# Two preactivated attention blocks on one core: the reciprocals of layer 1's softmax sums taken in a layout of 128 rows by 8

## The chip, the core and the metric

The kernel runs on one core of a Trainium2 chip. A core has TensorE (PE) for matrix products, VectorE (DVE) and ScalarE (ACT) for elementwise work, GpSimd (POOL) and SyncE (SP), which here mostly issue DMAs, a working memory of 128 partitions (SBUF), accumulator banks (PSUM) that PE writes, and DRAM. Each engine runs its own list of instructions in order; semaphores hold an instruction back until what it needs is done. The metric is the time of one execution on the device in microseconds (us), taken as the median of several runs.

## The reference

The input x is (4, 32, 32, 768) in fp32: four images of 1024 tokens and 768 channels. Two layers follow one another, each of them `x = x + attention(group_norm(x))`, with 12 heads of 64 channels. Cut to what matters, layer 1 is

```python
q, k, v = split(group_norm(x) @ w_qkv.T + b_qkv)        # per head
q, k, v = (layer_norm(dwconv3x3(a, w_pool)) for a in (q, k, v))
attn = softmax((q * scale) @ k.T + rel_h + rel_w)        # 1024 x 1024 per head
o = attn @ v + q
x = x + o @ w_proj.T + b_proj
```

Layer 0 has the same form without the convolution, the layer norms and the `+ q`. Softmax divides each row of exponentials by its sum. The kernel does this division after the product with v: one sum for each of 1024 queries and each head.

## The kernel before, in words

**Stages, pairs, chunks.** `stages` (L164) is the order of the eight passes: image 0 layer 0, image 1 layer 0, image 0 layer 1, image 1 layer 1, and the same for images 2 and 3. Each stage has six pairs of heads, hp 0 to 5; two heads of 64 channels fill the 128 partitions. `attend` (L720) works through a pair in two chunks c of QC = 512 queries, each with eight key tiles of 128. A chunk is 8 steps, a pair 16. In each half of a chunk PE computes four tiles of scores (L820: q times k; L822: the relative position bias), ACT takes the exponentials (L827), and PE multiplies them with V (L844) into the bank `av`.

**Order.** The program is written under a manual schedule: every engine's instructions stand exactly in the order in which the code issues them. `events` (L981) is a table from step to pieces of other work: the next pair's q, k and v (products L131, convolution taps on DVE L542 and L544, layer norm with sums by PE at L556 and L591, means and variances by DVE at L559 and L570, `r_ln` by L153 to L160, scaled V at L582, bias parts at L613 to L640), the next stage's group norm (mean by PE at L330, copied by DVE at L334 as `gmean`), and the last stage's projection with its `os_sums` (L902, L923). These pieces are issued between the steps of `attend`, so the tail of one chunk is woven into the next chunk and into this other work.

**What follows a chunk.** `rest` (L718) is a list of functions still to be done for a finished chunk. `more()` (L731) takes one from it and is called four times in a chunk: after the scores of the first half (step offset 0), after its product with V (offset 2), after the scores of the second half (offset 4) and after its product (offset 6). `landed` does nothing and lets one call pass. At offset 6 the new chunk's parts are put on the list and `copy` (L739) runs: ACT copies `av` to `weighed` (L742).

**Sums in layer 1.** V's last column of each head is replaced by ones (L584), so the last row of each head in `av` (rows 63 and 127) is the sum of exponentials. This is done for all chunks of layer 1 except the kernel's last (47 chunks, `by_ones`). POOL writes these two rows to DRAM as z (L748, 2x512) and reads them back as `t`, each repeated for the 64 rows of its head (L749, 128x512). In the following chunk:

- offset 0: `landed`;
- offset 2: `sums`: `restore_last` rebuilds the missing column of the product with V (PE L763, ACT L768, two DMAs by POOL L771), then ACT copies t with an accumulated sum (L784) and takes 1/t as exp(-ln t) (L792, L793); the accumulated sums of t and of its reciprocal go to `seen`, which the kernel's end reduces (L1057) and compares with a limit;
- offset 4: `result`: DVE refines the reciprocal with one Newton step (L800, L801), multiplies `weighed` by it (L804) and adds it into q (L805), which the projection reads in the next stage.

In a stage of layer 1 that is followed by one of layer 0, or by nothing (`short`, L211), the chunks (hp 4, c 1) and (hp 5, c 0) have one more `landed` ahead of `sums`. Layer 0 and the last chunk sum the exponentials on DVE (L836, L838) and PE (L789); their ACT copy is L790, and the last chunk's missing column comes back through the `whole` product.

**Buffers.** `weighed`, `t` and `inv` have one buffer each, z in DRAM has two. `small_bank` is a pool of PSUM banks taken in turn by short products.

Of the kernel before, what the change touches and what calls it, by code (L numbers as in the profile page):

```python
# [9 lines left out]
F32 = mybir.dt.float32  # L10
F32R = mybir.dt.float32r
I32 = mybir.dt.int32
AF = mybir.ActivationFunctionType
ALU = mybir.AluOpType
AX = mybir.AxisListType
PSUM = bass.MemoryType.PSUM

P = 128
B = 4
S = 32  # L20
T = S * S
C = 768
NC = C // P
D = 64
HALF = T // 2
QC = 512
# [7 lines left out]
LN = 75  # L34
# [3 lines left out]
IDENT, GROUP, CENTRE, HEADS, ONES, WHOLE = 0, P, 2 * P, 3 * P, 3 * P + 2, 3 * P + 2 + D  # L38
# [7 lines left out]
def two_layers(ctx: ExitStack, tc: tile.TileContext, keep, x_in, wqkv, wproj, rels, windows, vrow, small, const, onehot, picks, out):  # L46
# [19 lines left out]
    nc = tc.nc  # L66
    pool = lambda name, bufs, **kw: ctx.enter_context(tc.tile_pool(name=name, bufs=bufs, **kw))
    fixed = pool("fixed", 1)
    dram = pool("dram", 1, space=bass.MemoryType.DRAM)
    xnp = pool("xnp", 1)  # L70
    wp = pool("wp", 2)
    work = pool("work", 2)
    one = pool("one", 1)
    stat = pool("stat", 3)
# [50 lines left out]
    def small_bank(name):  # L125
        return ps_small.tile([P, 512], F32, tag="small", name=name)
# [14 lines left out]
    cst = fixed.tile([P, NCONST], F32, tag="cst", name="cst")  # L141
# [5 lines left out]
    def col(c, lo=0, hi=P):  # L147
        return sm[lo:hi, c : c + 1]
# [62 lines left out]
    def short(i):  # L211

        after = (i // NC + 1) * NC
        return items[i][1] == 1 and (after == len(items) or items[after][1] == 0)
# [150 lines left out]
    ones = fixed.tile([P, 2 * P], F32R, tag="ones", name="ones")  # L365
# [5 lines left out]
    seen = fixed.tile([P, 2 * len(items) * (T // QC)], F32, tag="seen", name="seen")  # L371
# [346 lines left out]
    rest, found = [], ()  # L718

    def attend(pair, os):  # L720


        q, k, bias = pair.q, pair.k, pair.bias


        by_ones = [pair.layer and (pair.i < len(items) - 1 or c < T // QC - 1) for c in range(T // QC)]
        os.append(q)
        nonlocal found
        heads = [slice(j * D, (j + 1) * D) for j in range(2)]

        def more():  # L731
            nonlocal found
            if rest:
                found = rest.pop(0)(*found)

        for c in range(T // QC):
            cols = slice(c * QC, (c + 1) * QC)

            def copy(av, ones=by_ones[c]):  # L739

                weighed = one.tile([P, QC], F32, tag="weighed", name="weighed")
                nc.scalar.copy(weighed, av)  # L742
                if not ones:
                    return weighed, acc
                t = work.tile([P, QC], F32, tag="t", name="t", bufs=1)

                z = dram.tile([2, QC], F32, tag="z", name="z", bufs=2)
                nc.gpsimd.dma_start(z, weighed[D - 1 :: D, :])  # L748
                nc.gpsimd.dma_start(t, z.unsqueeze(1).to_broadcast([2, D, QC]))  # L749
                return weighed, t  # L750

            def restore(weighed):

                ps = small_bank("whole")
                halves(ps, cst[:, WHOLE : WHOLE + P], weighed)
                nc.scalar.copy(weighed, ps)

            def restore_last(weighed):

                ps = small_bank("last")  # L760
                odd = cst[:, WHOLE + 1 : WHOLE + P : 2]
                for h in range(2):
                    nc.tensor.matmul(  # L763
                        ps[h * D : (h + 1) * D, : QC // 2], odd, weighed[:, h * (QC // 2) : (h + 1) * (QC // 2)],
                        start=True, stop=True,
                    )
                last = one.tile([P, QC // 2], F32, tag="last", name="last")
                nc.scalar.copy(last, ps[:, : QC // 2])  # L768
                for h in range(2):
                    rows = last[h * D + D // 2 - 1 : (h + 1) * D : D // 2, :]  # L770
                    nc.gpsimd.dma_start(weighed[D - 1 :: D, h * (QC // 2) : (h + 1) * (QC // 2)], rows)  # L771

            def landed(*found):

                return found

            def sums(weighed, of, c=c, ones=by_ones[c]):

                at = 2 * (pair.i * (T // QC) + c)
                inv = work.tile([P, QC], F32, tag="inv", name="inv", bufs=1)  # L780
                if ones:
                    t = of
                    restore_last(weighed)
                    nc.scalar.activation(inv, t, AF.Copy, accum_out=seen[:, at : at + 1])  # L784
                else:
                    z = small_bank("z")
                    t = work.tile([P, QC], F32, tag="t", name="t", bufs=1)
                    for j, rows in enumerate(heads):
                        nc.tensor.matmul(z[rows, :], cst[:, ONES : ONES + D], of[:, j, :], start=True, stop=True)  # L789
                    nc.scalar.activation(t, z, AF.Copy, accum_out=seen[:, at : at + 1])  # L790

                nc.scalar.activation(inv, t, AF.Ln, bias=tiny)  # L792
                nc.scalar.activation(inv, inv, AF.Exp, scale=-1.0, accum_out=seen[:, at + 1 : at + 2])  # L793
                if pair.layer and not ones:
                    restore(weighed)
                return weighed, t, inv

            def result(weighed, t, inv, cols=cols):

                nc.vector.scalar_tensor_tensor(t, t, -1.0, inv, ALU.mult, ALU.mult)  # L800
                nc.vector.scalar_tensor_tensor(inv, t, 2.0, inv, ALU.add, ALU.mult)  # L801

                if pair.layer:
                    nc.vector.tensor_tensor(inv, weighed, inv, ALU.mult)  # L804
                    nc.vector.scalar_tensor_tensor(q[:, cols], inv, col(LN + 4), q[:, cols], ALU.mult, ALU.add)  # L805
                else:
                    nc.vector.tensor_tensor(inv, weighed, inv, ALU.mult)
                return (inv,)

            def finish(inv, cols=cols):  # L810

                nc.scalar.activation(q[:, cols], inv, AF.Identity, bias=col(pair.column(2)))

            for g in range(0, NKT, 4):
                es = []
                for kt, place in zip(range(g, g + 4), (None, place_b, place_c, None)):
                    keys = slice(kt * P, (kt + 1) * P)
                    ps = place.pair("s") if place else ps_a.tile([P, 2, 512], F32, tag="a", name="s")
                    for j, rows in enumerate(heads):
                        nc.tensor.matmul(ps[:, j, :], k[rows, keys], q[rows, cols], start=True, stop=False)  # L820
                    for j, rows in enumerate(heads):
                        nc.tensor.matmul(  # L822
                            ps[:, j, :], ones[rows, kt % 2 * P : (kt % 2 + 1) * P], bias[c][rows, kt // 2, :],
                            start=False, stop=True,
                        )
                    e = work.tile([P, 2, QC], F32, tag="e", name="e", bufs=4)
                    nc.scalar.activation(e, ps, AF.Exp)  # L827
                    es.append(e)
                other_work(behind_scores)
                more()  # L830
                if g == 0:
                    av = ps_av.tile([P, QC], F32, tag="av", name="av")
                if not by_ones[c]:
                    if g == 0:
                        acc = work.tile([P, 2, QC], F32, tag="acc", name="acc", bufs=1)
                        nc.vector.tensor_tensor(acc, es[0], es[1], ALU.add)  # L836
                    for e in es[2 * (g == 0) :]:
                        nc.vector.tensor_tensor(acc, acc, e, ALU.add)  # L838
                yield
                yield  # L840
                for t, e in enumerate(es):
                    kt = g + t
                    for j in range(2):
                        nc.tensor.matmul(  # L844
                            av[j * D : (j + 1) * D, :], pair.vt[:, kt, j * D : (j + 1) * D], e[:, j, :],
                            start=(kt == 0), stop=(kt == NKT - 1),
                        )
                other_work(behind_av)
                more()
                if g + 4 == NKT:  # L850

                    n_parts = 2 if short(pair.i) and (pair.hp, c) in ((NC - 2, 1), (NC - 1, 0)) else 1
                    rest.extend((landed,) * n_parts + (sums, result) if pair.layer else (sums, result, finish))
                    found = copy(av)
                yield
                yield
# [161 lines left out]
    for k, stage in enumerate(stages):  # L1018
        call, sums, products = project(stage, oss[k])
# [346 lines left out]
```

## Time and profile before

| | before |
|---|---|
| median of 3 runs | 3814.33 us (3814.24 to 3817.77) |
| the profiled execution's own time | 3816.61 us |
| its span, first to last instruction | 3814.6 us |
| mean granted TensorE clock | 0.997 |
| PE busy | 3749.5 us (98%) |
| DVE busy | 2467.1 us (65%) |
| ACT busy | 1786.5 us (47%) |
| POOL busy | 529.1 us (14%) |
| moved by DMA | 330.44 MB, 87 GB/s |

The profile is one execution, recorded by the hardware. A group's row gives the line, the engine, the operation, output and input with their shapes, the number of instructions, then busy time in us and the mean duration of one in ns, then how long the engine was idle just before them and what ended that idle time. A line of the list of waits names an engine, the tile and line that waited, what it waited for, and us in total, the number of times and the longest. A timeline's line gives the start in us, the duration, engine, line and tile, and in brackets the idle time before it with what ended it. Idle time of an engine costs time only if the last engine to finish has to wait because of it.

### The profile page before, as it was taken

What the parts mean: (1) busy time and instruction counts of PE and PEld (TensorE: products, weight loads), DVE (VectorE), ACT (ScalarE), POOL (GpSimd) and SP (SyncE); (2) the same over time, 40 slices, a digit from 0 to 9 for tenths busy, and PEclk for the clock granted to TensorE, in tenths of its full rate; (3) what the DMA queues carried; (4) which work ended last, traced back from release to release, by engine and by line L of the source; (5) the groups of instructions that cost most, each with busy time, mean ns of one, the idle gap of its engine ahead of it and who ended that gap; (6) DMA issues with size and microseconds to landing.
All of it is one profiled execution on the core that took longest, in us unless ns stands there. A gap on an engine that the chain in (4) does not pass through costs nothing. (4 is left out here: it accounts for less than half of the span.)

```text
span 3814.6 us, 76313 instructions
## 1 busy us (share of the span) xinstructions
PE 3749.5 (98%) x32990; PEld 1656.7 (43%) x32990; DVE 2467.1 (65%) x3068; ACT 1786.5 (47%) x2573; POOL 529.1 (14%) x964
## 2 busy tenths in 40 slices
PE   8999999999999999999999999999999999999998
PEld 4535535533344443444535445355343444434442
DVE  2566554559678877688454554445686888867874
ACT  2455434545355553455534544254442555525562
POOL 0111100111111211111200010001111112111120
PEclk9999999999999999999999999999999999999999
DMA  4344443331431223311333132523114212142123
GB/s 152 102 122 116 134 144 90 101 81 40 119 102 48 57 59 95 123 48 48 82 111 121 53 78 63 171 61 78 46 46 131 87 50 66 47 122 65 48 58 100
DMA packets 214024, 330.44 MB, mean 87 GB/s; under 512 B 50390, under 2 KB 103698, under 8 KB 213680
## 3 DMA queue, kind: packets, MB, share of 16 engines
q1 hardware_dynamic: 122912, 211.86, 17.9%
q0 software_dynamic: 90768, 113.61, 12.6%
q8 instruction: 263, 4.31, 0.5%
q14 instruction: 81, 0.66, 0.1%
HBM read 184.23 MB, written 40.10 MB: 59 GB/s over the span
## 5 line engine op out<-in xcount | busy, mean ns | idle before, releaser
L827 ACT ACTIVATE e<-s 128x1024 f32<-128x1024 f32 x768 | 775.6, 1024 | 423.7 <-PE s L822 393.6
L131 PE MATMUL qkv<-xn,wqkv_t 128*64 128x512 f32 x3648 | 816.0, 596 | 7.0 <-DVE gmean L334 2.6
L820 PE MATMUL s<-q,k 64*128 64x512 f32 x3072 | 808.7, 603 | 6.6 <-ACT e L827 3.1
L544 DVE SCALAR_TENSOR_TENSOR shared<-shared,sm 128x1056 f32<-128x1056 f32 x576 | 757.9, 1316 | 15.7
L822 PE MATMUL s<-bias,ones 64*128 64x512 f32 x1536 | 611.7, 790 | 1.1 <-DMA bias<-whole 1.0
L844 PE MATMUL av<-e,vt 128*64 128x512 f32 x2624 | 596.2, 596 | 0.0
L131 PEld LDWEIGHTS qkv<-xn,wqkv_t 128*64 128x64 f32 x3648 | 256.5, 137 | 484.0 <-issue 466.1
L640 POOL DMA_DIRECT2D bias<-high x384 | 205.6, 556 | 1794.6 <-ACT high L629 1559.7
L838 DVE TENSOR_TENSOR acc<-acc,e 128x1024 f32<-128x1024 f32 x294 | 360.0, 1225 | 114.0 <-ACT e L827 87.4
L820 PEld LDWEIGHTS s<-q,k 64*128 64x128 f32 x3072 | 279.5, 186 | 264.4 <-issue 213.3
L527 ACT ACTIVATE shared<-qkv,sm 128x512 f32<-128x512 f32 (+1 forms) x288 | 129.3, 502 | 469.7 <-PE qkv L131 469.7
L844 PEld LDWEIGHTS av<-e,vt 128*64 128x64 f32 x2624 | 185.4, 137 | 350.9 <-issue 316.8
L822 PEld LDWEIGHTS s<-bias,ones 64*128 64x128 f32 x1536 | 148.6, 187 | 185.4 <-issue 184.1
L640 POOL DMA_DIRECT2D bias<-whole x384 | 207.2, 571 | 53.2 <-DVE whole L630 46.3
L836 DVE TENSOR_TENSOR acc<-e 128x1024 f32<-128x1024 f32 x49 | 60.0, 1225 | 215.4 <-ACT e L827 206.8
L742 ACT COPY weighed<-av 128x512 f32<-128x512 f32 x96 | 56.3, 587 | 279.0 <-PE av L844 270.1
L559 DVE TENSOR_REDUCE mean<-ln_c 128x8 f32<-128x512 f32 x144 | 98.6, 685 | 106.0 <-PE ln_c L556 106.0
L771 POOL DMA_DIRECT2D weighed<-last x94 | 50.7, 541 | 679.6 <-ACT last L768 638.6
L613 PEld LDWEIGHTS rel<-q,rel 64*32 64x32 f32 x6144 | 112.1, 106 | 68.6 <-issue 63.8
L613 PE MATMUL rel<-q_t,rel 64*32 64x32 f32 x6144 | 123.6, 195 | 1.8 <-issue 1.8
L613 PE MATMUL rel<-q,rel 64*32 64x32 f32 x6144 | 122.7, 195 | 1.9 <-issue 1.9
L412 DVE TENSOR_TENSOR shared<-shared,m3m 128x512 f32<-128x512 f32 x66 | 45.3, 687 | 119.9 <-PE m3m L131 119.8
(162 smaller groups left out, 4439.0 us busy)
## 6 DMA issues: line engine op xcount, KB each, us to landing
bias<-high POOLq DMA_DIRECT2D x384, 128.0 KB, 2.9
bias<-whole POOLq DMA_DIRECT2D x384, 128.0 KB, 3.0
wqkv_t<-in_wqkv SPq DMA_DIRECT2D x78, 384.0 KB, 3.2
wqkv_t<-mixed SPq DMA_DIRECT2D x66, 384.0 KB, 3.1
wproj_t<-mixed SPq DMA_DIRECT2D x48, 384.0 KB, 3.3
wqkv_t<-in_wqkv SPq DMA_DIRECT2D x66, 192.0 KB, 2.5
xn<-in_x SPq DMA_DIRECT2D x24, 512.0 KB, 7.7
x<-in_x SPq DMA_DIRECT2D x48, 256.0 KB, 3.2
```

What stands on the lines that cost most here:

```text
L131: nc.tensor.matmul(ps[lo : lo + D], a[:, lo : lo + D], b, start=start, stop=stop, **kw)
L527: nc.scalar.activation(self.pad[s][:, rows, there : there + src.shape[2]], src, AF.Identity, bias=col(self.column(s)))
L544: nc.vector.scalar_tensor_tensor(y, window, tap, y, ALU.mult, ALU.add)
L559: nc.vector.tensor_reduce(of, heads, AX.X, ALU.add)
L613: nc.tensor.matmul(ps[lo : lo + S, k * S : (k + 1) * S].rearrange("p (b c) -> p b c", b=2), rel[rows, 2 * self.layer + i, first : first + ...
L640: nc.gpsimd.dma_start(sets, some.unsqueeze(1).to_broadcast([D // 2, 2, QC]))
L820: nc.tensor.matmul(ps[:, j, :], k[rows, keys], q[rows, cols], start=True, stop=False)
L822: nc.tensor.matmul(ps[:, j, :], ones[rows, kt % 2 * P : (kt % 2 + 1) * P], bias[c][rows, kt // 2, :], start=False, stop=True,)
L827: nc.scalar.activation(e, ps, AF.Exp)
L836: nc.vector.tensor_tensor(acc, es[0], es[1], ALU.add)
L838: nc.vector.tensor_tensor(acc, acc, e, ALU.add)
L844: nc.tensor.matmul(av[j * D : (j + 1) * D, :], pair.vt[:, kt, j * D : (j + 1) * D], e[:, j, :], start=(kt == 0), stop=(kt == NKT - 1),)
```

## The change

In layer 1's 47 chunks ACT no longer takes the reciprocal, and DVE no longer refines it. `copy` (still at offset 6) writes the two rows of sums to DRAM as before and then reads them back as `z_inv[:, 0, :]`, 1024 numbers laid out as 128 rows by 8. A new part, `invert`, takes the reciprocal on DVE into `z_inv[:, 1, :]`, sums both along the 8 into `seen`, and has POOL write the reciprocals to DRAM (`inv`) and read them back as `t`, repeated for the 64 rows of each head. The last part, `weighed_result`, is two DVE instructions: `t = weighed * t`, and q plus t times the layer norm's weight. `weighed` gets two buffers.

The parts of a layer 1 chunk are now `landed` (offset 0), `invert` with `restore_last` (offset 2), `landed` (offset 4), `weighed_result` (offset 6, so two steps later than `result`; it is issued there before the new chunk's `copy`). For (hp 5, c 1) they are `invert`, `only_restore`, `weighed_result` at offsets 0, 2 and 4. In short stages (hp 4, c 1) and (hp 5, c 0) have `landed`, `invert`, `only_restore`, `weighed_result` at offsets 0, 2, 4 and 6. Layer 0 and the last chunk are as before. The orders of PE's and SP's instructions are the same before and after; ACT loses L784, L792 and L793 of these chunks, DVE loses four instructions a chunk and gets four, and POOL's one DMA t<-z becomes three: z_inv<-z, inv<-z_inv, t<-inv.

```diff
--- before.py
+++ after.py
@@ -738,16 +738,44 @@
 
             def copy(av, ones=by_ones[c]):
 
-                weighed = one.tile([P, QC], F32, tag="weighed", name="weighed")
+                weighed = one.tile([P, QC], F32, tag="weighed", name="weighed", bufs=2)
                 nc.scalar.copy(weighed, av)
                 if not ones:
                     return weighed, acc
+                few = 2 * QC // P
+                z = dram.tile([2, QC], F32, tag="z", name="z", bufs=2)
+                z_inv = stat.tile([P, 2, few], F32, tag="z_inv", name="z_inv")
+                nc.gpsimd.dma_start(z, weighed[D - 1 :: D, :])
+                nc.gpsimd.dma_start(z_inv[:, 0, :], z.rearrange("j (p x) -> (j p) x", x=few))
+                return weighed, z_inv
+
+            def invert(weighed, z_inv, c=c):
+
+                at = 2 * (pair.i * (T // QC) + c)
+                nc.vector.reciprocal(z_inv[:, 1, :], z_inv[:, 0, :])
+                nc.vector.tensor_reduce(seen[:, at : at + 2], z_inv, AX.X, ALU.add)
+                inv = dram.tile([2, QC], F32, tag="inv", name="inv", bufs=2)
+                nc.gpsimd.dma_start(inv.rearrange("j (p x) -> (j p) x", x=z_inv.shape[2]), z_inv[:, 1, :])
                 t = work.tile([P, QC], F32, tag="t", name="t", bufs=1)
-
-                z = dram.tile([2, QC], F32, tag="z", name="z", bufs=2)
-                nc.gpsimd.dma_start(z, weighed[D - 1 :: D, :])
-                nc.gpsimd.dma_start(t, z.unsqueeze(1).to_broadcast([2, D, QC]))
+                nc.gpsimd.dma_start(t, inv.unsqueeze(1).to_broadcast([2, D, QC]))
                 return weighed, t
+
+            def invert_and_restore(*found, invert=invert):
+
+                found = invert(*found)
+                restore_last(found[0])
+                return found
+
+            def only_restore(*found):
+
+                restore_last(found[0])
+                return found
+
+            def weighed_result(weighed, t, cols=cols):
+
+                nc.vector.tensor_tensor(t, weighed, t, ALU.mult)
+                nc.vector.scalar_tensor_tensor(q[:, cols], t, col(LN + 4), q[:, cols], ALU.mult, ALU.add)
+                return ()
 
             def restore(weighed):
 
@@ -774,24 +802,18 @@
 
                 return found
 
-            def sums(weighed, of, c=c, ones=by_ones[c]):
+            def sums(weighed, of, c=c):
 
                 at = 2 * (pair.i * (T // QC) + c)
                 inv = work.tile([P, QC], F32, tag="inv", name="inv", bufs=1)
-                if ones:
-                    t = of
-                    restore_last(weighed)
-                    nc.scalar.activation(inv, t, AF.Copy, accum_out=seen[:, at : at + 1])
-                else:
-                    z = small_bank("z")
-                    t = work.tile([P, QC], F32, tag="t", name="t", bufs=1)
-                    for j, rows in enumerate(heads):
-                        nc.tensor.matmul(z[rows, :], cst[:, ONES : ONES + D], of[:, j, :], start=True, stop=True)
-                    nc.scalar.activation(t, z, AF.Copy, accum_out=seen[:, at : at + 1])
-
+                z = small_bank("z")
+                t = work.tile([P, QC], F32, tag="t", name="t", bufs=1)
+                for j, rows in enumerate(heads):
+                    nc.tensor.matmul(z[rows, :], cst[:, ONES : ONES + D], of[:, j, :], start=True, stop=True)
+                nc.scalar.activation(t, z, AF.Copy, accum_out=seen[:, at : at + 1])
                 nc.scalar.activation(inv, t, AF.Ln, bias=tiny)
                 nc.scalar.activation(inv, inv, AF.Exp, scale=-1.0, accum_out=seen[:, at + 1 : at + 2])
-                if pair.layer and not ones:
+                if pair.layer:
                     restore(weighed)
                 return weighed, t, inv
 
@@ -849,8 +871,17 @@
                 more()
                 if g + 4 == NKT:
 
-                    n_parts = 2 if short(pair.i) and (pair.hp, c) in ((NC - 2, 1), (NC - 1, 0)) else 1
-                    rest.extend((landed,) * n_parts + (sums, result) if pair.layer else (sums, result, finish))
+                    if not pair.layer:
+                        parts = (sums, result, finish)
+                    elif not by_ones[c]:
+                        parts = (landed, sums, result)
+                    elif (pair.hp, c) == (NC - 1, 1):
+                        parts = (invert, only_restore, weighed_result)
+                    elif short(pair.i) and (pair.hp, c) in ((NC - 2, 1), (NC - 1, 0)):
+                        parts = (landed, invert, only_restore, weighed_result)
+                    else:
+                        parts = (landed, invert_and_restore, landed, weighed_result)
+                    rest.extend(parts)
                     found = copy(av)
                 yield
                 yield
```

## The prediction

> **What bounds the kernel now.** I read the shares of busy time first, then PE's waits, then the groups of the lines that the change touches, then the timelines around every place where one of those lines stands next to a wait of PE.
>
> ```profile
> PE 3749.5 (98%) x32990; PEld 1656.7 (43%) x32990; DVE 2467.1 (65%) x3068; ACT 1786.5 (47%) x2573; POOL 529.1 (14%) x964
> ```
>
> PE is idle for 3814.6 − 3749.5 = 65.1 us in all. The order of PE's instructions is the same before and after, matmul for matmul, so only these 65 us can shrink, and anything that makes PE wait adds to them. PE's list of waits says who sets them (waited for: total us, times, longest):
>
> ```profile
> PE warm L319 <- DMA rel<-in_windows: 12.9, 1, 12.9
> PE p1p L131 <- DVE os_sums L923: 7.4, 8, 1.6
> PE s L820 <- ACT e L827: 3.1, 3, 1.4
> ...
> PE qkv L131 <- DVE gmean L334: 2.6, 3, 0.9
> PE p3p L131 <- DVE os_sums L923: 1.9, 2, 1.1
> PE ln_t L591 <- DVE shared L582: 1.5, 3, 0.7
> ```
>
> None of these is a wait for a sum of exponentials or its reciprocal. What the change removes is therefore hidden work; it matters only where it stands just ahead of something PE waits for. The groups of the changed lines (count | busy us, mean ns | idle before them):
>
> ```profile
> L792 ACT ACTIVATE inv<-t,tiny 128x512 f32<-128x512 f32 x96 | 69.3, 722 | 3.1
> L793 ACT ACTIVATE inv<-inv 128x512 f32<-128x512 f32 x96 | 60.5, 630 | 3.0
> L784 ACT ACTIVATE inv<-t 128x512 f32<-128x512 f32 x47 | 29.8, 634 | 2.6 <-DMA t<-z 2.6
> L801 DVE SCALAR_TENSOR_TENSOR inv<-t,inv 128x512 f32<-128x512 f32 x96 | 66.4, 692 | 3.3
> L800 DVE SCALAR_TENSOR_TENSOR t<-t,inv 128x512 f32<-128x512 f32 x96 | 65.5, 682 | 10.5 <-ACT inv L793 10.5
> L804 DVE TENSOR_TENSOR inv<-weighed,inv 128x512 f32<-128x512 f32 x48 | 33.2, 692 | 1.7
> L805 DVE SCALAR_TENSOR_TENSOR q<-inv,sm,q 128x512 f32<-128x512 f32 x48 | 36.1, 751 | 1.8
> ```
>
> **What the Trainium skill says.** "Perfetto Trace Analysis", section "Tensor Engine Instruction (MATMUL, LD_WEIGHTS)", has ACT and DVE as strict first-in first-out engines; the trace agrees, since gaps such as the 2.28 us at L157 below are never filled by later work. "DMA: Bandwidth & Descriptors", section "Why a DMA increments its semaphore by 16 and not by 1", gives a transfer the largest number of engines up to 16 that divides the slowest dimension of both sides. In the trace of before the broadcast t<-z (outer dimension 2) is 64 packets of 4096 B, 159 ns each, over 5.6 us, which fits two engines, and it lands after 7.2/8.0/9.2 us (min/median/max). The new broadcast has the same shape. The 128×8 transfers should spread over 16. The same page, "Anatomy of one DMA — SWDGE (gpsimd) path", has about 2.0 us fixed; the trace's z<-weighed lands after a median of 1.7 us. "TensorE: Matmul & The Clock Gate", "Part 1: The HAM clock gate (the "warmup" mystery)", has PE at half rate after an idle window of about 3.4 us; the trace shows that after stalls of 2.63 and 0.77 us (1814.8 to 1819.6).
>
> **The change, part by part** (47 chunks: all of layer 1 but the kernel's last).
>
> *Removed from ACT*: L784, L792, L793 and two accumulator reads, 634 + 193 + 722 + 630 + 186 ns = 2.36 us × 47 = 111 us of busy time. ACT is 47% busy, and its exps wait for PE's scores (393.6 us of idle before L827), so 46 of the 47 give nothing. One does, see the short stages.
>
> *Removed from DVE*: L800 and L801, 1.37 us × 47 = 64.6 us. *Added*: a reciprocal of 128×8 and a sum over 128×2×8. Neither is in the trace; the nearest small rows take 170 ns (128×16), a 128×192 reduction 343 ns; I take 0.4 us for both, bounds 0.32 and 0.7, so 19 us. Net −46 us on an engine that is 65% busy.
>
> *Added on POOL*: two small DMA issues per chunk, each about 0.55 us as L748, on an engine 14% busy. Behind them on the queue stand the two DMAs of restore_last and, at least 10 us later, the bias DMAs (L640); the inserted issues and waits end about 5 us after the reciprocal. Worth 0; without that cover a late bias would hold up L822.
>
> *Does DVE wait for z_inv?* The reciprocal's slot lies typically 9.6 us, in the tightest chunks 4.5 to 6.4 us, after the time at which t<-z is issued now. I let z_inv land 2 us after issue (bounds 1.5 and 8, the latter if it spreads badly as t does): no wait. *Does the result wait for t?* From the reciprocal: 0.3, then inv to DRAM 2.1 (up to 4.5), then 8.0 (7.2 to 9.2): 10.5 to 13.5 us. The result's slot, moved from step offset 4 to 6, comes at least 16.8 us after the reciprocal in 42 of the 47 chunks; 13.6 us in two, 11.3 in one where DVE is idle, one more waits for another DMA anyway, and the tail is dealt with below. Worth 0, up to 3 us if all of it is late.
>
> *Moving the result.* L804's and L805's successors cost 0.692 + 0.751 = 1.44 us. Where they stood, freed DVE time is mostly swallowed by a wait for ACT, whose r_ln comes after the exps, which come after PE's scores:
>
> ```profile
> 1177.81 0.75 DVE L805 SCALAR_TENSOR_TENSOR q<-inv,sm,q 128x512 f32<-128x512 f32 x1
> 1180.84 0.17 DVE L157 TENSOR_TENSOR t_ln<-r_ln 128x16 f32<-128x16 f32 x1 [2.28 <-ACT r_ln L155]
> ...
> 1188.63 2.67 DVE L544 SCALAR_TENSOR_TENSOR shared<-shared,sm 128x1056 f32<-128x1056 f32 x2
> 1191.21 0.15 DVE L334 COPY gmean<-gn_mean 128x1 f32<-128x1 f32 x1
> ```
>
> From 1180.84 to 1191.21 DVE has no gap, and in the new order the two instructions stand between L544 and L334. PE waits for L334's small bank already:
>
> ```profile
> 1191.41 4.94 PE L131 MATMUL qkv<-xn,wqkv_t 128*64 128x512 f32 x22 [0.87 <-DVE gmean L334]
> ```
>
> This stall goes from 0.87 to 2.31 us. It stands at 1191, 1691 and 3079 us (first chunk of the third head pair of a layer-1 stage that has a next stage): **+1.44 × 3 = +4.3 us**.
>
> At 1266.7, 1766 and 3154.6 the pair comes before L570, and the gap behind it is only 0.74 us instead of 1.6 to 3.1, so V is ready 1.44 − 0.74 = 0.7 us late:
>
> ```profile
> 1271.48 0.17 DVE L157 TENSOR_TENSOR t_ln<-r_ln 128x16 f32<-128x16 f32 x1 [0.74 <-ACT r_ln L155]
> 1272.32 1.23 DVE L582 TENSOR_TENSOR vt<-shared,r_ln 128x1024 f32<-128x1024 f32 x1
> ```
>
> vt ends at about 1273.6, av starts at 1274.67 with some 0.8 us for signalling and exps between, so I charge 0.43 us each: **+1.3**. Elsewhere the gap absorbs it.
>
> Three stalls get shorter, because DVE has 1.44 us less ahead of them: two of 0.67 us for L582 (at 1449 and 3337), **−1.3**, and 1.08 us for L923 at 1949, **−1.1**.
>
> *Short stages* (no result is moved past an extra offset there). The one at 1811 is where ACT waits for the late t:
>
> ```profile
> 1811.12 0.63 ACT L784 ACTIVATE inv<-t 128x512 f32<-128x512 f32 x1 [2.61 <-DMA t<-z]
> ...
> 1817.46 1.13 PE L820 MATMUL s<-q,k 64*128 64x512 f32 x4 [2.63 <-ACT whole L619]
> ...
> 1819.59 2.08 PE L820 MATMUL s<-q,k 64*128 64x512 f32 x4 [0.77 <-ACT e L827]
> ...
> 1822.47 1.94 PE L556 MATMUL ln_c<-cst,shared 128*128 128x128 f32 x8 [0.38 <-DVE shared L544]
> ```
>
> ACT's wait goes and with it the 2.63; but the stall's place is taken by ln_c, which needs DVE's taps: L630 waits for ACT's and DVE's layer norm until 1816.1, the taps then run to 1820.0, so ln_c starts at 1820.2 instead of 1822.47: −2.3 at most, −0.9 if half of it is lost again in the following chain and −4 if the slow clock goes too. I take **−1.5**. The last short pair (3689 to 3713) is set by PE's own issue gap: **0**.
>
> *Tail.* t has one buffer, so ACT's copy of the last chunk's sums (L790, now at 3744.63, before it L742 that waited 2.25 us for L804) must wait until the last result has read it: t lands at 3743.5 to 3745.3, two instructions later it is free. PE's `whole` matmul, which takes the small bank that this copy frees and already waits 2.06 us for it, moves with it: **+0.8** (−0.5 to +2.5).
>
> Sum: +4.3 + 1.3 − 1.3 − 1.1 − 1.5 + 0 + 0.8 = **+2.5 us**. The profiled execution took 3816.6 us (span 3814.6 and 2.0 around it), and so would take 3819; it lies 2.3 us above the median of the three runs, 3814.33, from which I forecast **3817**. Differences below 0.2% (7.6 us: 3806.7 to 3822.0) can't be told from no change.
>
> **Rivals.**
> 1. *Slower: the longer gmean stalls drop PE's clock.* After 2.63 + 0.77 us of stall PE ran at half rate: 2.08 against 1.03 us for a tile's scores, 1.94 against 1.07 for ln_c, 4.30 against 3.65 for av, 2.6 us together. Three such: 2.5 + 7.8 = +10.3, **3825**. For it: that section says that the window runs freely, and 2.31 us lies near. Against: a stall of 1.88 us (at 913) left the clock whole. It decides if the length that suffices lies between 1.88 and 2.31.
> 2. *Faster: relief of ACT and DVE counts everywhere.* All layer-1 waits behind those engines go (2.63, 0.77, 0.43, about 0.9 more in the short stage, three of 0.87, two of 0.67, 1.08) and with them the slow clock, about 11 us, and the late place costs nothing: **3803**. Against: those waits end by chains that begin in PE's own scores.
> 3. *The transfers are late:* z_inv takes 8 us like t, and DVE waits 0.1 to 1.8 us in some six chunks; mostly swallowed, **3819**.
> 4. *Hidden altogether:* 3814, inside the forecast's own range.
>
> **Numbers.** Forecast with 4: 0.62, own range 3812 to 3821. Rival 1: 0.20 (3822 to 3829). Rival 2: 0.13. Rival 3: 0.05. Range 3808 to 3826, which leaves out most of rival 2 and the end of rival 1. Faster 0.13, same 0.67, slower 0.20.
>
> **What would show it.** Right: PE's waits for gmean total about 7 us for three; DVE idle before L157 grows; ACT busy falls to about 1676 us, DVE to about 2421; no wait for z_inv's DMA. Wrong: t's landing ending DVE waits; more than ten PE matmul groups at double time; a reciprocal far above 0.4 us; bias DMAs that end L822's waits.

## The result, and the profile after

The changed kernel takes **3822.97 us** (median of 18 runs, 3820.66 to 3826.18); the kernel before, run beside it, takes 3815.53 us (18 runs, 3813.20 to 3817.77). The ratio is 1.0020, 95% interval 1.0013 to 1.0026: slower by 7.4 us, just at the border of what the prediction called no change.

The first part of the page, busy time by engine, of the changed kernel (its profiled execution is the median one: 3822.97 us, span 3821.1 us):

```profile
PE 3754.2 (98%) x32990; PEld 1657.0 (43%) x32990; DVE 2415.1 (63%) x3068; ACT 1690.0 (44%) x2338; POOL 585.3 (15%) x1058
```

ACT lost 96 us and DVE 52 us of work, and the span is none the shorter for it. PE is busier by 4.7 us with the same matmuls: more of them ran at half rate, that is, each took twice as long for a while. PE's list of waits in the changed kernel (waited for: total us, times, longest):

```profile
PE qkv L131 <- DVE gmean L334: 6.8, 3, 2.3
...
PE whole L131 <- ACT t L813: 5.1, 1, 5.1
...
PE p3p L131 <- DVE os_sums L954: 0.9, 1, 0.9
```

The waits for gmean grew from 2.6 to 6.8 us and the wait in the tail from 2.1 to 5.1 us; those for L582 and for ACT's L619 are gone from the list, the one for os_sums is half.

PE's instructions stand in the same order in both kernels, so the start of each can be compared in the two traces. The lag of the changed kernel changes at these places and nearly nowhere else:

| us in the trace of before | what stands there | predicted, us | measured, us |
|---|---|---|---|
| 1191, 1691, 3079 | stalls for gmean | +4.3 | +4.2, and +3.4 of half rate after two of the three |
| 1274, 1774, 3162 | V late, av late | +1.3 | +0.7 |
| 1449, 3337 | waits for L582 gone | −1.3 | −1.7 |
| 1949 | wait for os_sums | −1.1 | −1.0 |
| 1812 to 1835 | short stage in the middle | −1.5 | −4.0 |
| 3689 to 3713 | last short pair | 0 | −0.8 |
| 3745 | tail | +0.8 | +3.0 of stall and +2.0 of half rate |
| 2803 | a stall of 1.87 us, the same in both | 0 | +1.6 of half rate |
| rest | start and small shifts | 0 | −1.0 |
| sum | | +2.5 | +6.4 (the spans differ by 6.5) |

DVE's timeline in the first of the three places, the two moved instructions between PE's product and gmean:

```profile
1190.36 0.68 DVE L776 TENSOR_TENSOR t<-weighed,t 128x512 f32<-128x512 f32 x1
1191.08 0.75 DVE L777 SCALAR_TENSOR_TENSOR q<-t,sm,q 128x512 f32<-128x512 f32 x1
1191.75 0.15 DVE L334 COPY gmean<-gn_mean 128x1 f32<-128x1 f32 x1
```

and PE's timeline in the first and the third:

```profile
1191.96 5.37 PE L131 MATMUL qkv<-xn,wqkv_t 128*64 128x512 f32 x24 [2.27 <-DVE gmean L334]
...
3080.36 7.07 PE L131 MATMUL qkv<-xn,wqkv_t 128*64 128x512 f32 x24 [2.27 <-DVE gmean L334]
```

The stall is 2.27 us in all three places, but the same 24 matmuls take 5.37 us in the first and 7.07 us in the third.

The timeline of the tail, on DVE, ACT and PE:

```profile
3747.30 0.69 DVE L776 TENSOR_TENSOR t<-weighed,t 128x512 f32<-128x512 f32 x1 [4.56 <-DMA weighed<-last]
3748.94 0.60 ACT L813 ACTIVATE t<-z 128x512 f32<-128x512 f32 x1 [4.58 <-DVE q L777]
3749.68 1.97 PE L131 MATMUL whole<-weighed,cst 128*64 128x512 f32 x4 [5.10 <-ACT t L813]
```

It is one chain. DVE waits for the restored column of `weighed`, which lands right behind t; ACT's copy waits for the one buffer t; PE waits for ACT, and its four matmuls then take 1.97 us. In the kernel before the same four wait less and take 1.08:

```profile
3745.37 1.08 PE L131 MATMUL whole<-weighed,cst 128*64 128x512 f32 x4 [2.06 <-ACT t L790]
```

### The profile page after: what moved, and what is told of

Same layout as the page of the kernel before. It is cut to its first block, busy times and chain, and to the rows that moved or that the text cites. A ratio compares the mean times of both kernels' runs of the same rounds, so it can differ in the third digit from the quotient of the medians.

```text
span 3821.1 us, 76370 instructions
## 1 busy us (share of the span) xinstructions
PE 3754.2 (98%) x32990; PEld 1657.0 (43%) x32990; DVE 2415.1 (63%) x3068; ACT 1690.0 (44%) x2338; POOL 585.3 (15%) x1058
## 4 chain that ended last, share of the span: by engine, by line
PE 88%; DVE 6%; issue 3%; ACT 1%; DMA 1%; POOL 1%; SPq 0%; DVEq 0%; ACTq 0%; POOLq 0%
PE qkv L131 19%; PE s L842 16%; PE av L866 15%; PE m4m L131 5%; PE m1m L131 4%; PE m3m L131 4%; PE s L844 4%; PE p3p L131 3%; PE p4p L131 3%; PE rel L613 3%; PE p1p L131 2%; PE m L131 2%; PE ln_c L556 1%; PE z L812 1%; DVE shared L544 1%
## 5 line engine op out<-in xcount | busy, mean ns | idle before, releaser
L131 PE MATMUL qkv<-xn,wqkv_t 128*64 128x512 f32 x3648 | 821.0, 599 | 11.3 <-DVE gmean L334 6.8
L131 PEld LDWEIGHTS qkv<-xn,wqkv_t 128*64 128x64 f32 x3648 | 257.4, 138 | 492.3 <-issue 470.9
L613 PEld LDWEIGHTS rel<-q,rel 64*32 64x32 f32 x6144 | 112.1, 106 | 68.7 <-issue 63.8
L157 DVE TENSOR_TENSOR t_ln<-r_ln 128x16 f32<-128x16 f32 x72 | 12.5, 174 | 187.2 <-ACT r_ln L155 187.2
L613 PE MATMUL rel<-q_t,rel 64*32 64x32 f32 x6144 | 123.7, 195 | 2.2 <-issue 2.2
L613 PE MATMUL rel<-q,rel 64*32 64x32 f32 x6144 | 122.7, 195 | 2.0 <-issue 2.0
```

What stands on the lines that cost most here:

```text
L131: nc.tensor.matmul(ps[lo : lo + D], a[:, lo : lo + D], b, start=start, stop=stop, **kw)
L613: nc.tensor.matmul(ps[lo : lo + S, k * S : (k + 1) * S].rearrange("p (b c) -> p b c", b=2), rel[rows, 2 * self.layer + i, first : first + ...
```

## The experiments

Each was timed together with the kernel before on the same chip (3815.3 us for e1 to e4, 3815.4 for e5 to e8, 3815.8 for e9 and e10); a ratio compares these two. Where a time is set against the changed kernel's 3822.97 us, the two were timed at different times, and the kernel before moved by up to 0.5 us between them. Diffs are shortened, "..." marks what is left out, and they are against the changed kernel unless the text says otherwise.

**e1_gmean_first: the two instructions behind gmean.**

```diff
 def landed(*found):
+    while deferred:
+        deferred.pop(0)()
     return found
...
-def weighed_result(weighed, t, cols=cols):
+def weighed_result(weighed, t, c=c, apply=apply):     # apply: the two instructions
+    if (pair.hp, c) == (2, 0) and pair.i // NC < len(stages) - 1:
+        deferred.append(lambda: apply(weighed, t))
+        return ()
+    apply(weighed, t)
```

> The changed kernel, but in three places (the first chunk of head pair 2 in the layer 1 stages that have a next stage) the two DVE instructions of weighed_result are held back until after the group norm's gmean copy and V's scaling. Theory: their place costs 1.4 us of stall three times, and in two of the three places PE's half rate afterwards 1.7 us more, so 7.6 us go: PE's wait for gmean back from 6.8 to about 2.6 us for three, time 3815.5 (3814 to 3817). Rival, the wait for gmean is DVE being late for another reason: time stays at 3823.

Measured: 3814.12 us (3811.15 to 3816.11), ratio to before 0.9996 (0.9987 to 1.0004): 8.9 us below the changed kernel. PE's timeline at the third place:

```profile
3073.46 5.37 PE L131 MATMUL qkv<-xn,wqkv_t 128*64 128x512 f32 x24 [0.88 <-DVE gmean L334]
```

The stall is 0.88 us again and the 24 matmuls take 5.37 us. In the trace the three places give back 1.4, 3.1 and 3.1 us, 7.6 in all, as the theory has it; why the medians give 1.3 us more is open. The place of six DVE instructions, 4.3 us of work, costs 7.6 us or a little more, and nothing at all a few instructions later.

**e2_own_t: another buffer for the last chunk's sums.**

```diff
-t = work.tile([P, QC], F32, tag="t", name="t", bufs=1)
+if pair.layer:
+    t = one.tile([P, T], F32, tag="q_t", name="q_t")[:, :QC]
+else:
+    t = work.tile([P, QC], F32, tag="t", name="t", bufs=1)
```

> The changed kernel, but the last chunk's sums are copied into another buffer than t, so that ACT does not wait for the last weighed_result. Theory 1, the one buffer is what costs 5 us at the end: PE's whole no longer waits 5.1 us, time 3818. Theory 2, the late landing of t and of the column behind it costs: DVE's weighed_result still waits until 3747, the sums that the projection reads still come after 3749.6, and PE's wait only changes its name: at most 1 to 2 us go, time 3821 to 3823.

Measured: 3817.91 us (3813.91 to 3821.12), ratio 1.0007 (1.0000 to 1.0014): 5.1 us below the changed kernel, theory 1. PE's timeline in the tail:

```profile
3745.34 1.08 PE L131 MATMUL whole<-weighed,cst 128*64 128x512 f32 x4 [0.79 <-ACT q_t L816]
3746.25 1.89 PE L131 MATMUL p4p<-os_sums,wproj_t 128*64 128x512 f32 x8
3749.60 1.08 PE L131 MATMUL p4p<-os_sums,wproj_t 128*64 128x512 f32 x4 [1.47 <-DVE os_sums L936]
```

DVE still waits 4.56 us and its weighed_result still starts at 3747.27, as theory 2 had it. But PE reads the late sums only after twelve other matmuls, and what is left is a stall of 1.47 us at full rate instead of one of 5.10 us with half rate behind it.

**e3_per_head: t read back by two DMAs of 64 rows.**

```diff
-nc.gpsimd.dma_start(t, inv.unsqueeze(1).to_broadcast([2, D, QC]))
+for j in range(2):
+    nc.gpsimd.dma_start(t[j * D : (j + 1) * D, :], inv[j : j + 1, :].to_broadcast([D, QC]))
```

> The changed kernel, but t is read back by two DMAs, one for each head (64 rows from one), instead of one with an outer dimension of 2. Theory: the 7.8 us to landing come from two engines moving 64 packets; with 64 as outer dimension each lands in 2 to 3 us, the column that follows in the queue lands in 1.7 instead of 6.8 us, the tail's wait of 5.1 us falls to about 1 and its half rate goes: time 3818 (3817 to 3819.5); the three waits for gmean stay 2.27 us. Rival, the broadcast takes 8 us whatever its outer dimension: both still land after about 8 us, time 3823 or a little more.

Measured: 3822.36 us (3820.78 to 3825.91), ratio 1.0020 (1.0011 to 1.0028), so no gain that shows. Times from issue to landing (min/median/max), of t<-inv and then of weighed<-last, in the changed kernel:

```profile
DMA to landing us min/median/max: 7.2/7.8/8.8
DMA to landing us min/median/max: 1.6/6.8/8.3
```

and the same two in e3:

```profile
DMA to landing us min/median/max: 2.7/2.9/4.2
DMA to landing us min/median/max: 1.6/2.5/3.9
```

t is slow by its shape, as the theory says: 2.9 instead of 7.8 us, and the column behind it 2.5 instead of 6.8. The edit changes the outer dimension and also makes two DMAs of one; two alone was not tried, but the 64 packets of 4096 B start within a median of 1.45 us here and 5.44 us in the changed kernel, more than the halving that I would expect of a second DMA of the same kind. But the expected time was wrong, because another wait took the place in the tail. POOL's timeline in the tail, at the second DMA of the column:

```profile
3743.54 0.55 POOL L800 DMA_DIRECT2D weighed<-last  x1 [2.90 <-PE z L813]
```

In the changed kernel both were issued by 3741.9; here the second waits for PE, lands at 3745.13, and PE's wait for ACT is still 4.18 us, with half rate behind it. Why POOL waits for so late a matmul is open.

**e4_move_only: the kernel before with the move alone.** Against the kernel before:

```diff
-weighed = one.tile([P, QC], F32, tag="weighed", name="weighed")
+weighed = one.tile([P, QC], F32, tag="weighed", name="weighed", bufs=2)
...
-parts = (landed, sums, result)
+parts = (landed, sums, result, apply)   # result: Newton step; apply: L804, L805
```

> The kernel before (ACT's reciprocals, DVE's Newton step, one broadcast), with only the last two DVE instructions of result moved from offset 4 to 6 and weighed in two buffers. Theory, the move is what costs: three waits for gmean of 2.3 us instead of 0.87, with PE's half rate after one to three of them, less 1 to 2 us for the two shorter waits for L582 and one for os_sums: before plus 4 to 8 us, 3820 to 3823. Rival, the cost lies in the new layout's transfers: before plus 0 to 2 us, 3816 to 3817.

Measured: 3818.08 us (3814.78 to 3821.07), ratio 1.0007 (0.9998 to 1.0015): below the expected time. In its profile the three waits for gmean are 6.8 us, with half rate after two of them: +3.1, +3.1 and +1.4 us, as in the changed kernel. The shorter waits for L582 and os_sums, which I had charged to the move, do not appear. They could not: in the chunks ahead of them neither this edit nor the change moves the result, and what the changed kernel lacks there is the Newton step (L800 and L801 stand at 1434.71 and 1931.69 us in the trace of before). In the tail this kernel is some 3 us ahead of the kernel before: 1.2 us because with two buffers for `weighed` ACT no longer waits for L804, and 1.8 above all because half rate at 3760 is absent in this profile. The theory's cost is in the trace, but the second buffer, an effect of the edit that the theory left out, takes 1.2 us off the time; the median alone would not have told the two.

**e5_early_own: the result back at offset 4.** As e3, with the edit of e2, and

```diff
-parts = (landed, invert_and_restore, landed, weighed_result)
+parts = (landed, invert_and_restore, weighed_result)
```

> The changed kernel with t read back by one DMA for each head, weighed_result back at offset 4 (parts landed, invert with restore_last, weighed_result), and the last chunk's sums in another buffer than t. Theory, the cost of the change is the late place and the end, and the late place was forced only by t's 7.8 us: t lands 6 us after the reciprocal, the slots at offset 4 are at least 8 us after it, so no wait of DVE for a DMA in the general chunks; the three waits for gmean 0.87 us; the gains (4 us at 1812, 1 at 1947) stay: 3810 (3807 to 3812). Rival, DVE then waits for the restored column or for t: waits of DVE for a DMA in many chunks and a time of 3816 or more.

Measured: 3808.19 us (3804.67 to 3814.67), ratio 0.9979 (0.9973 to 0.9986): faster than the kernel before by 7 us. The waits for gmean are 2.7 us for three. DVE waits for the restored column in four places, and for t nowhere:

```profile
DVE t L777 <- DMA weighed<-last: 14.3, 4, 9.1
```

The late place had been paid for a transfer that two DMAs bring in 2.9 us. One part of the expectation failed: in this profile only 1.3 of the 4 us at 1812 stay, since a stall of 2.13 us has half rate behind it there:

```profile
1818.52 1.94 PE L556 MATMUL ln_c<-cst,shared 128*128 128x128 f32 x8 [2.13 <-DVE shared L544]
```

**e6_one_chunk: the new method in one chunk.** Against the kernel before: the method's functions, used only where

```diff
+new = (pair.i, c) == (3 * NC + 4, 0)
```

> The kernel before with the new method in one of its 47 chunks, the first chunk of head pair 4 of image 1's layer 1 (the one whose late t made ACT wait 2.61 us). Theory, the 4 us that the changed kernel gains between 1812 and 1826 us come from this chunk alone: before minus 4, 3811 (3810 to 3813), no wait of PE for whole L619. Rival, the gain there needs the relief of the neighbours: before minus 0 to 1.5.

Measured: 3810.03 us (3807.25 to 3813.64), ratio 0.9988 (0.9981 to 0.9995). In the trace the 4.0 us are gained between 1800 and 1835 us, and nothing before. PE's timeline there:

```profile
1817.04 1.13 PE L853 MATMUL s<-q,k 64*128 64x512 f32 x4 [0.40 <-ACT e L860]
...
1819.95 1.06 PE L556 MATMUL ln_c<-cst,shared 128*128 128x128 f32 x8 [1.55 <-ACT ln_ln L153]
1820.94 3.65 PE L877 MATMUL av<-e,vt 128*64 128x512 f32 x16
```

ln_c starts at 1819.95 (the prediction said 1820.2), and av takes 3.65 us, not 4.30. A second part, 1.2 us, comes in the tail from the two buffers of `weighed`: PE's wait of 2.06 us is 0.86 us here. The two make 5.2 us, and the medians differ by 5.4.

**e7_both: the edits of e1 and e2 together.**

> The changed kernel with both edits that took time off it: the three weighed_results behind gmean and V's scaling, and the last chunk's sums in another buffer. Theory, the two costs are independent: 8.9 and 5.1 us below 3823, so 3809 (3807 to 3811) and faster than the kernel before by 6 us. Rival, they share one cause (the end waits for what the earlier stalls delay): no more than 9 us below, 3814.

Measured: 3807.72 us (3806.48 to 3811.88), ratio 0.9981 (0.9975 to 0.9988), 15.3 us below the changed kernel; 8.9 and 5.1 make 14.0. The two costs add up, which the rival of one shared cause (no more than 9 us) does not allow, and without them the change is a gain of 7.7 us.

**e8_half_behind: a stall of 1.5 us.** As e1, but the multiplication stays ahead of gmean and only the addition into q is held back:

```diff
 nc.vector.tensor_tensor(t, weighed, t, ALU.mult)
-nc.vector.scalar_tensor_tensor(q[:, cols], t, col(LN + 4), q[:, cols], ALU.mult, ALU.add)
+if (pair.hp, c) == (2, 0) and pair.i // NC < len(stages) - 1:
+    deferred.append(lambda: add_to_q(t))
+else:
+    add_to_q(t)
```

> The changed kernel with, in the three places, only the second of the two DVE instructions (the one that adds into q) held back behind gmean: PE's three waits are then about 1.5 us instead of 2.27. Theory 1, a stall of that length leaves PE's clock whole: 2.2 us of stall and about 3.4 to 5 us of half rate go, 3816.5 (3815.5 to 3818). Theory 2, what decides is where the stall falls and not whether it is 1.5 or 2.3 us: half rate still follows in two of three, 3820.5.

Measured: 3815.83 us (3813.99 to 3818.16), ratio 1.0001 (0.9992 to 1.0009), 7.1 us below the changed kernel, for 0.75 us less of DVE's work in front of each gmean. From PE's list of waits:

```profile
PE qkv L131 <- DVE gmean L334: 4.5, 3, 1.5
```

No stall of the three had half rate behind it: theory 1.

**e9_work_back: the removed work put back.** e7_both, with work that the output doesn't need, in the 40 chunks whose second part is `invert_and_restore`:

```diff
+nc.scalar.activation(again, cst[:, :QC], AF.Copy, accum_out=scrap[:, 0:1])
+nc.scalar.activation(again, again, AF.Copy)
+nc.scalar.activation(again, again, AF.Copy, accum_out=scrap[:, 1:2])
...
+nc.vector.scalar_tensor_tensor(again, again, -1.0, again, ALU.mult, ALU.mult)
+nc.vector.scalar_tensor_tensor(again, again, 2.0, again, ALU.add, ALU.mult)
```

> e7_both with work put back on ACT and DVE that does nothing for the output: in 40 of the 47 chunks three ACT instructions on 128x512 with two accumulator reads at the place of the removed ones (some 85 us of busy time, on a constant, so that they wait for no DMA) and two DVE instructions at the place of the Newton step (55 us). Theory, the 140 us of relief are hidden but for single places: two waits for L582 of 0.7 us come back and in the chunk at 1812 ACT is 2.2 us later again, so 1.5 to 4 us above e7, 3809 to 3812. Rival 1, the relief counts everywhere: 8 us or more above e7, 3816. Rival 2, it is worth nothing anywhere: 3808.

Measured: 3810.00 us (3807.35 to 3813.63), ratio 0.9986 (0.9979 to 0.9992), which overlaps that of e7. Its busy times:

```profile
PE 3747.3 (98%) x32990; PEld 1655.4 (43%) x32990; DVE 2464.5 (65%) x3148; ACT 1768.3 (46%) x2538; POOL 585.7 (15%) x1058
```

ACT (1691.2 us in e7) has 77 and DVE (2415.4) 49 us more. Up to 3700 us its trace lags e7's by no more than 0.8 us, at the end by 2.9, of which 1.7 are half rate after a stall in the tail. So 126 us of work cost at most the 2.3 us between the medians: rival 1 is out. Of the 4.0 us at 1812, 3.8 stay, though ACT's work there is back: they came from ACT's wait for t, not from its instructions. The two waits for L582 that I expected back stay away, but nothing was put back there: the chunks ahead of 1449, 1949 and 3337 us are among the seven that e9 leaves as they are. So e9 doesn't speak of these three places, where the work taken off DVE is worth 2.7 us.

**e10_both_per_head: e7 with two DMAs for t.**

> e7_both with t read back by one DMA for each head. Theory: t and the column behind it land 5 us sooner, which only DVE's wait at the end can use: PE's wait for os_sums in the tail (1.2 us) goes, 3806.5 (3805 to 3808). Rival, as with one broadcast: 3807.7; with the 47 additional issues in the way of the bias DMAs it would be 3809 or more.

Measured: 3808.85 us (3806.11 to 3811.78), ratio 0.9982 (0.9975 to 0.9989): the same as e7. The wait for os_sums in the tail, which was to go, fell from 1.18 to 0.56 us, without an effect on the time that shows; the 47 additional issues cost nothing that shows either.

**Half rate by length of stall.** The twelve profiles (before, after, e1 to e10) have the same matmuls in the same order, so I took as normal the shortest distance between the starts of each two neighbours in any profile, and summed what the 6 us after a stall took beyond it. Over the stalls that end in L131, in L591 or in the matmul of `good` near the end (L1061 in the kernel before):

| stall | profiles x places | followed by a loss over 0.9 us |
|---|---|---|
| 1.4 to 1.7 us | 52 | 0 |
| 1.7 to 2.1 us | 38 | 17 |
| 2.1 to 2.4 us | 12 | 8 |
| over 4 us | 4 | 4 |

Where there is a loss it is near 1.7 us up to 2.4 us, and 1.7 to 2.1 us above. The same stall of 1.88 us at 913 us has it in five profiles and not in seven. Stalls ahead of other lines, above all L556 and L613 in the short stages, follow one another closely and are not in the table; there half rate came once after a stall of only 1.52 us (e4, at 1829), and the loss in e5 at 1818 was 3.0 us.

The length of the stall alone doesn't decide, and the record of the granted clock in the traces says what does. In all twelve profiles half rate comes in stretches of 3.41 us, at times two in a row, and within a profile all of them start a whole number of 3.413 us apart, to within 5 ns. So PE's time can be cut into windows of that length. Of some 13,200 such windows at full clock after the first 25 us, all 31 in which PE had no matmul for 1.98 us or more were followed by one at half rate, 16 of the 30 with 1.72 to 1.98 us were, and none of the others. The first two stalls of 2.27 us in the changed kernel, cut into these windows (start:end and length in us; busy us of PE, PEld, DVE, ACT and POOL; granted clock; share and GB/s of the DMA engines):

```profile
1187.00:1190.41 3.41, 2.69 (x18) 1.36 (x14) 3.34 (x5) 1.70 (x3) 3.25 (x7) 1.00 1.00 255
1190.41:1193.82 3.41, 1.86 (x10) 0.72 (x12) 3.27 (x8) 1.27 (x2) 0.58 (x1) 1.00 0.31 72
1688.76:1692.17 3.41, 1.14 (x11) 0.90 (x11) 3.27 (x7) 2.72 (x4) 1.50 (x3) 1.00 0.86 197
1692.17:1695.58 3.41, 3.41 (x10) 0.97 (x8) 3.37 (x4) 0.00 (x0) 0.00 (x0) 0.50 0.02 5
```

The first stall is split by the end of a window, 0.72 and 1.55 us, and keeps its clock; the second falls whole into one, and so does the third (3077.98 to 3081.39). A window at half rate does half of 3.41 us of work, which is the loss of 1.7 us. And a stall of 1.88 us has to fall whole into a window, for which the chance is (3.41 − 1.88) / 3.41 = 0.45 if it may fall anywhere, an estimate from these figures; 17 of 38, stalls of 1.87 to 2.06 us, are 0.45.

That agrees with what the Trainium skill says in "TensorE: Matmul & The Clock Gate", "Part 1: The HAM clock gate (the "warmup" mystery)": the activity window runs freely, so where a stall falls in it counts. Its idle window of about 3.4 us is not the stall that is needed, though: 1.9 us can be enough here.

## Why the prediction was right, and where it was wrong

The time lies in the stated range (3808 to 3826), but it is slower than the forecast of 3817 by 6 us and outside the forecast's own range (3812 to 3821). In the prediction's own terms it lies where rival 1 was put (3822 to 3829), at 0.20, and rival 1's mechanism ran. That rival 1's number came so near is in part luck: its half rate was priced at 7.8 us, of which about 3.4 came, and the tail, which it didn't have, brought 4.3 more. By the prediction's steps:

1. *Removed work is hidden.* Right in the main: e9 puts back 126 us for at most 2.3. In three places, at 1449, 1949 and 3337, the Newton step that is gone is worth 2.7 us. The prediction had these gains, as 2.4 us, but under the move of the result, which is not made in the chunks concerned. ACT lost 96 us and not 111, because the durations of instructions that follow one another overlap in the trace (L784 at 3722.88 for 0.64 us, its accumulator read at 3723.41).
2. *New operations.* Reciprocal 195 ns and sum 170 ns, 0.37 us against 0.4. z_inv landed after 1.9 us against 2, and DVE waited for it once, 3.2 us, near the end. (The 1.7 us given there for z<-weighed is that of the column; z<-weighed has a median of 1.6.)
3. *Moving the result.* The place and the size of the stall, 1.40 us three times for 1.44, were right; e1 and e4 show it from both sides. V's lateness cost 0.7 in place of 1.3 us.
4. *Half rate.* This is the step that failed, and by a misreading. I argued against rival 1 that a stall of 1.88 us at 913 left the clock whole. The timeline of PE in the kernel before says the opposite:

```profile
913.24 0.63 PE L591 MATMUL ln_t<-cst,shared 128*128 128x128 f32 x4 [1.88 <-DVE shared L560]
913.79 6.64 PE L131 MATMUL qkv<-xn,wqkv_t 128*64 128x512 f32 x22
```

22 of the same matmuls take 4.94 us at 1191, and the record of the granted clock shows 0.50 in the window behind the stall:

```profile
914.32:917.73 3.41, 3.41 (x12) 0.97 (x10) 3.31 (x3) 1.30 (x2) 0.62 (x2) 0.50 0.69 174
```

So a stall of 1.88 us can suffice, and the three lengthened stalls (2.27 us) should have been charged about two thirds (8 of 12 in the table) of 1.7 us each, +3.4. Rival 1's price of 2.6 us was that of a stretch of two windows, 1818.85 to 1825.68 us; after the gmean stalls it is one. And 2803 us shows that a stall that no change touches gives or takes 1.7 us between two profiles.
5. *Short stage.* Right in mechanism, mis-sized: −4.0, the far end of what I allowed. I had kept the slow clock under ln_c and av; it is gone from there. In the changed kernel's trace half rate comes earlier, behind a stall of 2.22 us at 1815, and is swallowed by the wait ahead of ln_c, which takes 1.06 us and av 3.65:

```profile
1823.01 1.06 PE L556 MATMUL ln_c<-cst,shared 128*128 128x128 f32 x8 [1.09 <-ACT e L849]
1824.00 3.65 PE L866 MATMUL av<-e,vt 128*64 128x512 f32 x16
```

In e5 it came later and cost some 2.7 of the 4.0 us.
6. *Last short pair.* 0 forecast, −0.8 in the trace; the cause is open.
7. *Tail.* The buffer was named, its price was wrong: +5.1 against +0.8 (up to +2.5). Two terms were missing. t landed at 3746.87 instead of 3743.5 to 3745.3, since DVE had waited 7.2 us for the column of the chunk before, which came behind its t, and reached the reciprocal only at 3736.73; and behind a wait of 5.1 us PE is at half rate, 2.0 us. e2 takes 5.1 us away in the medians and 4.7 in the trace. The restored column, which lands after 1.7 us in the kernel before, lands after 6.8 because it is issued behind t; it came 0.35 us after t here and so added little.

With 3.4 for half rate after gmean, 5.1 for the tail and −4.0 for the short stage the sum is 2.5 + 3.4 + 4.3 − 2.5 = 7.7 us, against 7.4 between the medians. That it fits so closely is chance: the smaller differences of the table (V, L582, the last short pair, the start) take off some 3 us more, and half rate at 2803, 1.6 us, comes and goes. That the forecast missed by no more than 6 us is in part luck too: of the 7.7 us that it lacked for half rate and the tail, the short stage paid 2.5.

Of the rivals that did not come, rival 2's terms add up to about 12 us and not 11; e9 rejects it either way.

## What to carry to other kernels

When one engine is 98% busy, work taken off the others is worth what the waits of that engine say and nothing else; what the change moves has to be followed to the next instruction that the busy engine waits for, here a copy of one column. In this kernel a stall of the matmul engine that grows past some 1.8 us can cost 1.7 us more than its length, and it is the idle time within one window of 3.41 us that counts. So a stall is worth cutting below that even where it can't be removed, as e8 shows with 1.5 us, and one such event in a single profile need not be an effect of the change. If a slow transfer is the reason for a late place, look first at the transfer's shape: here one DMA for two heads against one for each.

## What the runs showed of the hardware that I had not expected

- Half rate can follow a stall of 1.87 us and depends on when it falls (17 of 38 stalls of 1.7 to 2.1 us; none of 52 of 1.4 to 1.7 us at the places of the table). It comes in windows of 3.41 us after a window with 1.72 us or more without a matmul (all 31 with 1.98 or more, 16 of 30 below that), and costs about 1.7 us for each.
- A small DMA issued behind a broadcast with an outer dimension of 2 landed only when that one had: 90 of the 94 DMAs of the column in the changed kernel were issued while t was under way, and landed 0.17 to 0.54 us after it. The median is 6.8 us, and 1.7 us in the kernel before, where t had mostly landed. As two DMAs with 64 as the outer dimension the broadcast takes 2.9 us instead of 7.8, and the column 2.5.
